# Four graph layers on one core: layer 2's edge records in rows of 512 bytes instead of 264, and a smaller fill of their table

## The chip, the cores and the metric

One of the cores of a Trainium2 chip runs the whole program; the other cores are idle. The metric is the device time of one execution in microseconds. The kernel before was timed three times; beside that there is one profiled execution, from which every duration below is taken.

## The reference

Four graph layers run one after the other on 3125 nodes of 256 features and 53125 edges (25000 random ones, the same reversed, and a loop on each node), sorted by their second endpoint. Each layer is `x = x + layer(relu(layernorm(x)))`:

- layer 0: for each edge, a two-layer perceptron on both endpoints' features and the 64 edge attributes, summed by endpoint; then an update perceptron and a norm;
- layer 1: attention of 4 heads over the edges of a node, with a 64-wide vector for each of 64 edge types, softmax by node;
- layer 2: attention of 8 heads, with `key = k[src] + edge_attr @ We`. Here the softmax runs over all edges at once, and the sum goes to the endpoint by which the edges are *not* sorted:

```python
dst = edge_index[0]
src = edge_index[1]
e = (edge_attr @ We + be).reshape(-1, H, C)
key_j = k[src] + e
alpha = (q[dst] * key_j).sum(-1) / math.sqrt(C)
alpha = jax.nn.softmax(alpha, axis=0)
out = v[src] * alpha[:, :, None]
out = jax.ops.segment_sum(out, dst, num_segments=n)
```

- layer 3: single-head attention with a loop on each node, softmax by node, then a gated cell.

Everything is float32.

## The kernel before

**Stages.** `prelude` builds lists: it counts the edges of each node, ranks the nodes by degree, writes layer 0's table `s_l0_src` (`a_d`, L366) and computes, for every edge, a place in layer 2's table (`t.row2`, L555). At its end a flag says whether the inputs fit the fixed sizes; `tile_gnn_kernel` loads it on every engine and runs `by_slots` where they fit and another function, `by_blocks`, where they don't. `by_slots` then does layer 0 (tile pools `s_e0`), layer 1 (`s_e1`), layer 2 (`s_e2`), the node work before layer 3 (`s_n3`) and layer 3 (`s_e3`). Nodes go in 25 blocks of 128.

**Transfers by index.** Rows of DRAM tables are fetched and stored by indirect DMAs on GpSimd's (POOL's) queue, one index for each of 128 partitions. All go through `Kit.gather` (L154) and `Kit.scatter` (L158); `Kit.queued` keeps their order on POOL as written. The views of the profile tell them apart by the tile: `gt` is layer 0's, `kv<-s_l_kv` layer 1's, `kv<-s_l_rows` layer 2's, `xg` layer 3's; `st` and `s_nodes` belong to the lists, and `out_dram` is the final store, whose last one has 53 rows.

**The records.** Layer 2 needs the edges by their *other* endpoint, in 25 blocks of 128 sources. A block has room for 18 x 128 edges (`TILES`; the last one 8 x 128). For each edge a record is written to its place in the DRAM table `s_src_records` (`ss`): 64 attributes, the offset of the first endpoint's row, and the source's number within its block, 66 floats. The edges are taken 125 at a time, one for each of 125 partitions, in 425 scatters. `loaded` (L588) fetches the attributes for five scatters into one of two buffers `rec`, `filled` writes the two other columns on VectorE (DVE, L592 and L593), and `scatter_src` issues the scatter. These 425 steps are strewn between the gathers of other layers: one after each pair of `gt` gathers of layer 0 from the second block of nodes on, 25 after that, and two after each group of up to four gathers of layer 1.

Places that no edge takes must hold a source number of -1. So the whole table is filled beforehand, on SP's queue, from a constant `sfill`:

```python
for i in range(40):
    nc.sync.dma_start(ss[i * 11 * P:(i + 1) * 11 * P, :].rearrange("(p r) c -> p (r c)", p=P),
                      sfill.rearrange("p r c -> p (r c)"))
```

Behind it on SP's queue stand the stores of `a_d` (L366).

**Layer 2** loads one block of records at a time (`opened`, L1180), into one of two buffers `srec`; each partition reads its 18 records as one run. DVE copies out the row offsets (`dst`, L1183), the source numbers (L1185) and their negatives (L1187), and ScalarE the attributes (L1210). The offsets are the indices of the gathers of `kv`, issued eight pairs of tiles ahead (`fetched`). Two transposed weights of layer 3 are prepared at the start of the same stage, through the same PSUM bank as the first block's attributes (L1156 to L1161).

**What orders the work.** Layer 0 runs on a hand-made clock of ticks, layers 1 to 3 as generators that are stepped in turn. Engines run their own instructions in order; a recording layer puts in the waits. `sync` DMAs go out on SP's queue in the recorded order.

Of the kernel before, what the change touches and what calls it, by code (L numbers as in the profile page):

```python
# [9 lines left out]
F32 = mybir.dt.float32  # L10
# [3 lines left out]
ALU = mybir.AluOpType  # L14
# [4 lines left out]
P = 128  # L19
N = 3125  # L20
NB = 25
# [3 lines left out]
EP, EC = 125, 425  # L25
D = 256
# [4 lines left out]
NT = 440  # L31
# [3 lines left out]
SREC = 66  # L35
# [10 lines left out]
assert HM >= HALF[0]  # L46

TILES = (18,) * (NB - 1) + (8,)
TM = TILES[0]
FR = mybir.dt.float32r  # L50
assert sum(TILES) == NT
XH = 516
KVQ = 1024
XPR = 514
# [188 lines left out]
def prelude(ctx, tc, a, a_d, nodes_d, ss, st_d, flag, t):  # L243
# [3 lines left out]
    nc = tc.nc  # L247
    c = ctx.enter_context(tc.tile_pool(name="pc", bufs=1))
    wk = ctx.enter_context(tc.tile_pool(name="pw", bufs=2))
# [4 lines left out]
    nc.sync.dma_start(dst_i, a["dst"].rearrange("(p c) -> p c", c=EC))  # L254
    xh = c.tile([P, NB, XH], F32, name="xh")
    for b0 in range(0, NB - 1, 6):
# [16 lines left out]
    b1 = k.load_row(c, a["L0_gnn_eb1"], "b1", parts=1)  # L273


    sfill = c.tile([P, 11, SREC], F32, name="sfill")
    nc.gpsimd.memset(sfill, 0.0)
    nc.gpsimd.memset(sfill[:, :, 65:66], -1.0)
    nid = c.tile([P, NB], F32, name="nid")
# [7 lines left out]
    cap = c.tile([P, NB], F32, name="cap")  # L287
    nc.gpsimd.memset(cap, float(P * TM))
    nc.gpsimd.memset(cap[:, NB - 1:NB], float(P * TILES[NB - 1]))
    none = c.tile([1, 512], F32, name="none")  # L290
    nc.gpsimd.memset(none, -BIG)
    last = c.tile([P, NB], F32, name="last")
# [8 lines left out]

    nc.scalar.dma_start(a_d[NP:NP + 1, :], none)

    for i in range(40):
        nc.sync.dma_start(ss[i * 11 * P:(i + 1) * 11 * P, :].rearrange("(p r) c -> p (r c)", p=P),
                          sfill.rearrange("p r c -> p (r c)"))

    both_e = c.tile([EP, EC, 2], I32, name="both_e")
    nc.gpsimd.tensor_copy(both_e[:, :, 0], e_src)
# [161 lines left out]
    pc2, pv = pc3[:, 0:2, :], pc3[0:1, 2, :]  # L471
# [8 lines left out]
    nc.vector.tensor_reduce(v2, most, AX.X, ALU.add)  # L480
    over = c.tile([P, NB], F32, name="over")
    nc.vector.tensor_tensor(over, pc2[:, 1, :], cap, ALU.is_gt)
    v3 = c.tile([P, 1], F32, name="v3")
    nc.vector.tensor_reduce(v3, over, AX.X, ALU.add)
    nc.tensor.matmul(pv[:, 0:1], v1, k.ones[:EP, 0:1], start=True, stop=False)
# [65 lines left out]
    step = wk.tile([EP, EC], F32, name="step", tag="edge", bufs=4)  # L551
    nc.vector.tensor_scalar(step, eq[:, NB - 1, :], float(TILES[NB - 1] - TM), float(TM), op0=ALU.mult, op1=ALU.add)
    nc.vector.tensor_tensor(step, step, pa_i, ALU.mult)
    nc.vector.tensor_tensor(step, step, pj_i, ALU.add)
    nc.vector.scalar_tensor_tensor(t.row2, hs, float(P * TM), step, op0=ALU.mult, op1=ALU.add)  # L555
    nc.vector.tensor_scalar(t.dst_e, dst_i, float(KVQ), None, op0=ALU.mult)
# [3 lines left out]
def by_slots(ctx, tc, a, out, a_d, nodes_d, ss, t):  # L560
    nc = tc.nc
# [17 lines left out]
    srcb, ai, row2, dst_e, srcl_e = t.srcb, t.ai, t.row2, t.dst_e, t.srcl_e  # L579
    attr = a["edge_attr_64"].rearrange("(p c) k -> p c k", c=EC)  # L580
    CH = 5
    recs = ctx.enter_context(tc.tile_pool(name="s_recs", bufs=2))
    done = [0]

    def loaded(c):

        rec = recs.tile([EP, CH, SREC], F32, name="rec")
        nc.sync.dma_start(rec[:, :, 0:64], attr[:, c:c + CH, :])  # L588
        return rec

    def filled(c, rec):
        nc.vector.tensor_copy(rec[:, :, 64], dst_e[:, c:c + CH])  # L592
        nc.vector.tensor_copy(rec[:, :, 65], srcl_e[:, c:c + CH])  # L593
# [3 lines left out]
    def scatter_src(n):  # L597

        for _ in range(n):
            c = done[0]  # L600
            if c == EC:
                return
            c0 = c - c % CH
            if c == 0:
                rec_of[0] = loaded(0)
                filled(0, rec_of[0])
            if c % CH == 1 and c0 + CH < EC:
                rec_of[c0 + CH] = loaded(c0 + CH)
            if c % CH == 3 and c0 + CH < EC:
                filled(c0 + CH, rec_of[c0 + CH])  # L610
            k.scatter(ss, row2[:, c:c + 1], rec_of[c0][:, c % CH, :], "src_records")
            done[0] += 1


    qpool = ctx.enter_context(tc.tile_pool(name="s_q", bufs=1))
    qtab = qpool.tile([P, NB, D], F32, name="qtab", tag="qtab")
    with tc.tile_pool(name="s_e0", bufs=2) as wk, tc.tile_pool(name="s_e0w", bufs=1) as w, \
            tc.tile_pool(name="s_e0p", bufs=2, space=PSUM) as ps:
        w1b = k.load_w(w, a["L0_gnn_eW1"][D:2 * D, :], "w1b")
# [302 lines left out]
        for i in range(-9, len(pairs)):  # L922
            if i >= 0:
                b, s = pairs[i]
# [24 lines left out]
    with tc.tile_pool(name="s_e1", bufs=2) as wk, tc.tile_pool(name="s_e1w", bufs=1) as w, \  # L949
# [144 lines left out]
        def step(ns, nl):  # L1094

            for todo, n in ((soon, ns), (calm, nl)):
                for _ in range(n):
                    if todo and next(todo[0], todo) is todo:
                        todo.pop(0)
            for t in list(late1):  # L1100
                t[0] -= 1
                if t[0] <= 0:
                    late1.remove(t)
                    t[1]()
# [17 lines left out]
        while soon or calm or late1:  # L1122
            step(1, 1)
    scatter_src(EC)

# [17 lines left out]
    with tc.tile_pool(name="s_e2", bufs=2) as wk, tc.tile_pool(name="s_e2w", bufs=1) as w, \  # L1145
# [28 lines left out]
        def opened(b):  # L1174

            o = Block()
            o.b, o.n = b, TILES[b]
            r0 = b * P * TM
            o.rec = wk.tile([P, TM, SREC], F32, name="srec")
            nc.sync.dma_start(o.rec[:, 0:o.n, :].rearrange("p j c -> p (j c)"),  # L1180
                              ss[r0:r0 + o.n * P, :].rearrange("(p j) c -> p (j c)", j=o.n))
            o.dst = wk.tile([P, TM], I32, name="dst2")
            nc.vector.tensor_copy(o.dst[:, 0:o.n], o.rec[:, 0:o.n, 64])  # L1183
            o.slb = wk.tile([P, TM], BF, name="slb")
            nc.vector.tensor_copy(o.slb[:, 0:o.n], o.rec[:, 0:o.n, 65])  # L1185
            o.nsl = wk.tile([P, TM], F32, name="nsl")
            nc.vector.tensor_scalar(o.nsl[:, 0:o.n], o.rec[:, 0:o.n, 65], -1.0, None, op0=ALU.mult)  # L1187
            o.sc = wk.tile([P, TM, 8], F32, name="sc")
            o.kv, o.oh = [], {}

            qt = wk.tile([P, D], F32, name="qt", bufs=1)
            nc.vector.tensor_scalar(qt.bitcast(I32), q2[:, b, :].bitcast(I32), -4096, None, op0=ALU.bitwise_and)
            o.qh = wk.tile([P, D], FR, name="qh")
            nc.scalar.copy(o.qh, qt)
            o.ql = wk.tile([P, D], FR, name="ql")
            nc.vector.tensor_sub(o.ql, q2[:, b, :], qt)
            return o
# [85 lines left out]

        pairs = [(b, j) for b in range(NB) for j in range(0, TILES[b], 2)]
        AHEAD = 8
        blocks = {0: opened(0)}
        for b, j in pairs[:AHEAD]:
            fetched(blocks[b], j)
        ready = turned(blocks[0], 0)
        soon = []  # L1290
        for i, (b, j) in enumerate(pairs):
            o = blocks[b]
            if j == 2 and b + 1 < NB:
                blocks[b + 1] = opened(b + 1)
            if j == 4:

                nc.sync.dma_start(q2[:, b, :], kvq_d[b * P:(b + 1) * P, 768:KVQ])
            eat, oht = ready if j % T6 == 0 else (eat, oht)
            scored(o, j, eat, oht, j % T6 // 2)
            if j % T6 == 2 or (j % T6 == 0 and j + 2 == o.n):  # L1300
                j2 = j - j % T6 + T6
                if j2 < o.n:
                    ready = turned(o, j2)
                elif b + 1 < NB:
                    ready = turned(blocks[b + 1], 0)
            for g in list(soon):
                if next(g, soon) is soon:
                    soon.remove(g)
            if j + 2 == o.n:
                soon.append(weighed(o))  # L1310
            if i + AHEAD < len(pairs):
                b2_, jn = pairs[i + AHEAD]
                fetched(blocks[b2_], jn)
# [1015 lines left out]
def kernel(tc: tile.TileContext, a: dict, out: bass.AP):  # L2329
    nc = tc.nc  # L2330
    a_d = nc.dram_tensor("s_l0_src", [NP + 1, 512], F32, kind="Internal").ap()
    nodes_d = nc.dram_tensor("s_nodes", [NP, XH], F32, kind="Internal").ap()
    ss = nc.dram_tensor("s_src_records", [NT * P, SREC], F32, kind="Internal").ap()
    st_d = nc.dram_tensor("s_src_type", [2 * E], I32, kind="Internal").ap()
    with tc.tile_pool(name="flags", bufs=1) as flags:
        flag = flags.tile([1, 1], I32, name="flag")
        with tc.tile_pool(name="keep", bufs=1) as keep:
            t = Lists(keep)
            prelude(tc, a, a_d, nodes_d, ss, st_d, flag, t)
            _, v = nc.values_load_multi_w_load_instructions(  # L2340
                flag, engines=[ET.PE, ET.DVE, ET.Activation, ET.Pool, ET.SP], min_val=0, max_val=1,
                skip_runtime_bounds_check_because="a comparison's result")
            with tc.If(v[0] == 1):
                by_slots(tc, a, out, a_d, nodes_d, ss, t)
        with tc.If(v[0] == 0):
            by_blocks(tc, a, out)
# [31 lines left out]
```

## Time and profile before

| | us |
|---|---|
| median of 3 runs | 3944.12 (3943.7 to 3950.05) |
| the profiled execution | 3928.64 |
| its span, first to last instruction | 3926.8 |
| PE, DVE, ACT, POOL busy | 2369.8, 2388.1, 1092.7, 2576.2 |
| the 425 record scatters on POOL | 526.6 busy, 1239 ns mean |

The page gives for each engine its busy time; a share of the whole span is a mean over stages that have different limits. A line of a group or of a tile names the source line, the engine, the operation, `out<-in`, the count and the time. A line of waits reads "engine line `<-` what it waited for: us in all, times, longest". In the table of stretches each line is one stretch of the span. "Issue" is time in which an engine waited for nothing that the profile shows. The profiled execution lies 0.4% below the median of the runs, so differences are taken within it.

### The profile page before, as it was taken

The page shows a single profiled execution, that of the slowest core. Times are in us where ns is not written, and L with a number is a line of the kernel's source. Part 1 is how long each engine was busy: PE and PEld are TensorE (multiplying, and loading weights), DVE is VectorE, ACT ScalarE, POOL GpSimd, SP SyncE. Part 2 cuts the span into 40 slices and gives each one's busy share as a digit, 9 for nine tenths or more (in the row PEclk, how much of TensorE's full clock was granted, in tenths as well). Part 3 has the DMA queues.
Part 4 walks back from the last instruction along what each step waited for, and adds up shares of the span by engine and source line. Part 5 has one row for each costly group of instructions (what it writes and reads, how often), then busy time and mean ns, then how long its engine had stood idle before and what let it go on. Part 6 is the DMA issues. An engine that isn't in the chain of part 4 may idle for free. (4 is left out here: it accounts for less than half of the span.)

```text
span 3926.8 us, 32540 instructions
## 1 busy us (share of the span) xinstructions
PE 2369.8 (60%) x9174; PEld 1477.2 (38%) x9174; DVE 2388.1 (61%) x4836; ACT 1092.7 (28%) x2294; POOL 2576.2 (66%) x2497
## 2 busy tenths in 40 slices
PE   5726688878887725354656467699889931121223
PEld 4313244434443424343444355466666630010111
DVE  5646557656575345565656677688989943444444
ACT  1111112212221121121212222566766621011222
POOL 3447777777777067777777763576776626666765
PEclk9868889889898956566667578799999965555556
DMA  6345556566564154555555563666666533333332
GB/s 217 125 140 170 157 155 186 160 175 171 164 177 126 61 169 136 142 154 156 160 148 170 159 187 126 223 209 198 211 208 205 165 106 94 97 92 96 103 100 76
DMA packets 295839, 595.89 MB, mean 152 GB/s; under 512 B 113501, under 2 KB 154508, under 8 KB 295650
## 3 DMA queue, kind: packets, MB, share of 16 engines
q0 software_dynamic: 163616, 472.86, 40.7%
q1 hardware_dynamic: 131512, 119.79, 10.2%
q8 instruction: 76, 1.25, 0.1%
q10 hardware_dynamic: 522, 1.06, 0.1%
q14 instruction: 113, 0.93, 0.1%
HBM read 510.85 MB, written 82.21 MB: 151 GB/s over the span
## 5 line engine op out<-in xcount | busy, mean ns | idle before, releaser
L158 POOL DMA_INDIRECT s_src_records<-rec,row x425 | 526.6, 1239 | 135.9 <-issue 121.8
L154 POOL DMA_INDIRECT kv<-s_l_rows,dst x440 | 456.6, 1038 | 208.9 <-issue 71.9
L154 POOL DMA_INDIRECT kv<-s_l_kv,st x439 | 481.7, 1097 | 167.5 <-issue 120.4
L920 PE MATMUL ph<-wm,st 128*128 128x512 f32 x904 | 477.3, 657 | 150.4 <-DVE acc L939 101.5
L154 POOL DMA_INDIRECT gt<-s_l_src,srcb x452 | 433.8, 960 | 168.2 <-issue 106.3
L154 POOL DMA_INDIRECT xg<-s_l_rows,src x439 | 430.8, 981 | 133.7 <-issue 133.7
L986 PE MATMUL pk<-rel,toh 64*128 64x64 f32 x878 | 183.6, 374 | 367.9 <-DVE mk L988 248.8
L134 PE MATMUL pt<-ident,hb 128*128 128x128 f32 x50 | 17.0, 442 | 555.5 <-ACT hb L1428 555.5
L934 DVE TENSOR_TENSOR ph<-gt,ph 128x1024 f32<-128x1024 f32 x226 | 276.7, 1225 | 122.9 <-PE ph L920 96.3
L988 DVE TENSOR_TENSOR mk<-kv,pk 128x1024 f32<-128x1024 f32 (+3 forms) x119 | 135.2, 1136 | 344.8 <-DMA kv<-s_l_kv,st 330.0
L986 PEld LDWEIGHTS pk<-rel,toh 64*128 64x128 f32 x878 | 165.9, 279 | 401.2 <-issue 348.3
L920 PEld LDWEIGHTS ph<-wm,st 128*128 128x128 f32 x904 | 177.9, 209 | 363.4 <-issue 296.3
L1027 PE MATMUL acc<-kv,ident 128*128 128x256 f32 x878 | 241.6, 442 | 62.3 <-DVE kv L1023 62.3
L981 ACT ACTIVATE toh<-tb,negp 64x512 f32<-64x512 f32 (+3 forms) x119 | 81.9, 688 | 693.3 <-PE pk L986 643.3
L1279 PE MATMUL pg<-kv,oh 128*128 128x256 f32 x880 | 248.8, 408 | 3.7 <-DVE kv L1276 3.4
L939 DVE SCALAR_TENSOR_TENSOR acc<-ph,acc 128x1024 f32<-128x1024 f32 x201 | 245.2, 1220 | 3.6
L1027 PEld LDWEIGHTS acc<-kv,ident 128*128 128x128 f32 x878 | 195.6, 226 | 102.0 <-DVE kv L1023 67.8
L134 PEld LDWEIGHTS pt<-ident,hb 128*128 128x128 f32 x50 | 7.2, 202 | 583.2 <-ACT hb L1428 583.2
L1464 DVE TENSOR_SCALAR sc<-xg,own 128x4 f32<-128x4 f32 (+3 forms) x119 | 30.7, 258 | 322.0 <-DMA xg<-s_l_rows,src 314.8
L1421 DVE SCALAR_TENSOR_TENSOR acc<-xg,sc,acc 128x256 f32<-128x256 f32 x439 | 210.9, 484 | 7.9
L1234 PE MATMUL pk<-we,eat 64*128 64x256 f32 x880 | 162.0, 441 | 45.4 <-DVE mk L1240 43.4
L1240 DVE TENSOR_TENSOR mk<-kv,pk 128x512 f32<-128x512 f32 x220 | 149.6, 680 | 44.2 <-DMA kv<-s_l_rows,dst 38.7
(373 smaller groups left out, 5275.2 us busy)
## 6 DMA issues: line engine op xcount, KB each, us to landing
s_src_records<-sfill SPq DMA_DIRECT2D x40, 363.0 KB
srec<-s_src_records SPq DMA_DIRECT2D x24, 594.0 KB
rec<-in_edge_attr_dram SPq DMA_DIRECT2D x85, 156.2 KB
tb<-s_slot_types SPq DMA_DIRECT2D x101, 128.0 KB
gt<-s_l_src,srcb POOLq DMA_INDIRECT x452, 3.5
kv<-s_l_rows,dst POOLq DMA_INDIRECT x440, 3.8
kv<-s_l_kv,st POOLq DMA_INDIRECT x439, 4.0
xg<-s_l_rows,src POOLq DMA_INDIRECT x439, 2.8
```

The source lines that it names most:

```text
L154: self.queued(lambda: self.nc.gpsimd.indirect_dma_start(out=to, out_offset=None, in_=table, in_offset=bass.IndirectOffsetOnAxis(ap=index, ...
L158: st = self.queued(lambda: self.nc.gpsimd.indirect_dma_start(out=table, out_offset=bass.IndirectOffsetOnAxis(ap=index, axis=0), in_=rows, ...
L920: nc.tensor.matmul(ph[:, h, :], stat[h][:, s % 4, :], ms[b][h], start=True, stop=True)
L934: nc.vector.tensor_add(ph, gt, ph)
L939: nc.vector.scalar_tensor_tensor(accs[b], ph, 0.0, accs[b], op0=ALU.max, op1=ALU.add)
L986: nc.tensor.matmul(pk[:, q, :], toh[:, q, :], rel, start=True, stop=True)
L988: nc.vector.tensor_tensor(mk[:, 0:n].rearrange("p s (h d) -> p s h d", h=4), kv[:, 0:n, 0:D].rearrange("p s (h d) -> p s h d", h=4), pk[:, ...
L1027: nc.tensor.matmul(acc, ident, v[:, q, :], start=(s0 + q == 0), stop=(s0 + q == C - 1))
L1234: nc.tensor.matmul(pk[:, i, :], eat[i * 64:(i + 1) * 64, q, :], we[i * 64:(i + 1) * 64, :], start=True, stop=True)
L1240: nc.vector.tensor_add(mk, o.kv[j // 2][:, :, 0:D], pk)
L1279: nc.tensor.matmul(pg, oh[:, j % T6 + i, :], v[:, i, :], start=(j + i == 0), stop=(j + i == n - 1))
L1421: nc.vector.scalar_tensor_tensor(acc, xgs[q // U3][:, q % U3, 0:D], s[:, q:q + 1], acc, op0=ALU.mult, op1=ALU.add)
```

## The change

A record becomes 128 floats, 512 bytes, of which the last 62 are zeros. The two record buffers become two named tiles whose unused columns are cleared once at the start of `by_slots`; they are given back after the last scatter, ahead of layer 2. The block loads of layer 2 take the wider rows. The fill covers only the last three of each block's 18 (the last block's 8) places of every partition, in three DMAs, and a new test makes a block with fewer edges than the unfilled places hold (15 x 128, in the last block 5 x 128) a violation, which clears the flag. In the inputs a block of sources has 2089 to 2233 edges, the last one 881.

```diff
+FULL = (15,) * (NB - 1) + (5,)
+SW = 128
...
-    sfill = c.tile([P, 11, SREC], F32, name="sfill")
+    sfill = c.tile([P, 3, SW], F32, name="sfill")
...
+    low = c.tile([P, NB], F32, name="low")
+    nc.gpsimd.memset(low, float(P * FULL[0]))
+    nc.gpsimd.memset(low[:, NB - 1:NB], float(P * FULL[NB - 1]))
...
-    for i in range(40):
-        nc.sync.dma_start(ss[i * 11 * P:(i + 1) * 11 * P, :].rearrange("(p r) c -> p (r c)", p=P),
-                          sfill.rearrange("p r c -> p (r c)"))
+    for b0, b1_ in ((0, 12), (12, NB - 1), (NB - 1, NB)):
+        n = TILES[b0]
+        r0 = b0 * P * TM
+        nc.sync.dma_start(ss[r0:r0 + (b1_ - b0) * P * n, :].rearrange("(b p j) c -> p b (j c)", p=P, j=n)
+                          [:, :, FULL[b0] * SW:n * SW],
+                          sfill.rearrange("p r c -> p (r c)")[:, None, :].to_broadcast([P, b1_ - b0, 3 * SW]))
...
     nc.vector.tensor_tensor(over, pc2[:, 1, :], cap, ALU.is_gt)
+    nc.vector.tensor_tensor(low, low, pc2[:, 1, :], ALU.is_gt)
+    nc.vector.tensor_add(over, over, low)
...
-    recs = ctx.enter_context(tc.tile_pool(name="s_recs", bufs=2))
+    qpool = ctx.enter_context(tc.tile_pool(name="s_q", bufs=1))
+    qtab = qpool.tile([P, NB, D], F32, name="qtab", tag="qtab")
+    begun = ExitStack()
+    recs = begun.enter_context(tc.tile_pool(name="s_recs", bufs=1))
+    ring_ = [recs.tile([EP, CH, SW], F32, name=f"rec{i}") for i in range(2)]
+    for rec in ring_:
+        nc.vector.memset(rec[:, :, SREC:SW], 0.0)
...
-        rec = recs.tile([EP, CH, SREC], F32, name="rec")
+        rec = ring_[c // CH % 2]
...
     scatter_src(EC)
+    begun.close()
...
-            o.rec = wk.tile([P, TM, SREC], F32, name="srec")
+            o.rec = wk.tile([P, TM, SW], F32, name="srec")
...
-    ss = nc.dram_tensor("s_src_records", [NT * P, SREC], F32, kind="Internal").ap()
+    ss = nc.dram_tensor("s_src_records", [NT * P, SW], F32, kind="Internal").ap()
```

In the two programs' lists of instructions POOL has the same order but for its memsets, and DVE the same but for the two operations of the new test, the two clearings, and the first record columns, which are written earlier. On SP the fill's 37 stores are gone, and in layer 2 the load of the second block stands behind two loads of weights instead of in front of them. PE and ScalarE have small exchanges of neighbours in the lists' stage and at the start of layer 2.

## The prediction

> **What bounds the kernel now.** I read the page's busy row first. No engine passes 66% of the span, so the average says little and the change has to be priced stage by stage. I cut the span where the names of GpSimd's (POOL's) transfers change: lists up to 237 us, layer 0 (`gt` gathers) 314 to 1236, layer 1 (`kv<-s_l_kv`) 1391 to 2255 with its tail to 2467, layer 2 (`kv<-s_l_rows`) 2467 to 3123, layer 3 (`xg`) from 3206. The table of stretches (columns: stretch, its length, busy us and count for each engine, clock, DMA share, GB/s) then answers for each:
>
> ```profile
> 314.00:1236.00 922.00, 739.88 (x2123) 366.21 (x2123) 574.88 (x782) 191.26 (x390) 708.24 (x684) 0.89 0.59 167
> 1391.00:2255.00 864.00, 440.11 (x1630) 346.75 (x1630) 498.05 (x791) 180.03 (x286) 648.80 (x565) 0.64 0.55 157
> 2467.00:3123.00 656.00, 579.62 (x3309) 407.62 (x3309) 575.97 (x1151) 440.93 (x1005) 455.73 (x440) 0.96 0.65 207
> ```
>
> POOL is busy 708 of 922 us in layer 0, and its waits there say why it is not 922: after each of its 684 transfers stand about 0.3 us "issue" in which it waits for nobody. The groups of layer 0 on POOL give 60.6 + 96.6 + 11.9 + 4.6 = 174 us of that, so 882 of 922 us are POOL going as fast as it can. In layer 1 it is 649 + 155 of 864. Both stages that carry the scatter of records are therefore set by POOL's time per transfer, not by bytes: the DMA engines stand at 0.59 and 0.55. Layer 2, which loads the records, is different: PE 580 and DVE 576 of 656 us, POOL has room.
>
> So three prices matter: POOL's time for one scatter, what waits for its landing, and the block loads of layer 2. The next rows are from the views of single tiles (form, count, minimum/median/maximum in ns):
>
> ```profile
> L158 POOL DMA_INDIRECT s_src_records<-rec,row x425: 1172/1210/2279, 314.6 to 2254.2; - x142
> L154 POOL DMA_INDIRECT st<-s_src_type,off_i x25: 940/944/11131, 172.2 to 213.4; - x25
> L158 POOL DMA_INDIRECT s_nodes<-xh,rank_i x25: 956/960/4613, 130.7 to 164.7; - x25
> L158 POOL DMA_INDIRECT s_l_rows<-row,nid_i x25: 950/987/1890, 1748.3 to 2457.4; - x25
> 3918.40 1.57 POOL L158 DMA_INDIRECT out_dram<-gg,nid_i  x1 [7.03 <-issue]
> ```
>
> The record scatter costs 1.21 us where the others cost 0.94 to 0.99. Is that its short row (264 bytes) or its 125 rows instead of 128? `st` moves 72 to 288 bytes a row, 128 rows, and costs 0.944. `s_l_rows` moves 4096 bytes a row, 128 rows, and costs 0.987. The last line is the final store, 53 rows of 1024 bytes: 1.57. The price follows the number of rows, not their length, and the change keeps 125.
>
> **The change part by part.** The sum is made against the profiled execution, 3928.64 us (span 3926.8); it lies 15.5 us (0.4%) under the median 3944.12, and I carry the difference over to the median.
>
> *The scatter, 425 on POOL.* Row 264 to 512 bytes. By length alone, from 944 (at most 288 bytes) to 987 (4096): 43 ns over 3808 bytes, so 248 bytes are 3 ns, x 425 = 1.2 us. The bounds: a gain of 1210 - 960 = 250 ns each if shortness were the cause, 399 of them in layers 0 and 1, -100 us; a loss of the whole 43 ns each, 425 x 0.043 = +18 us. I take +1, nearest to `st`, whose rows are the only others that short.
>
> Here two rules of the Trainium skill pull apart, both on the page DMA: Bandwidth & Descriptors. "Specifications" says that a transfer under 512 bytes makes the DMA engine read, modify and write; if that were in the 1.21 us, the estimate would be the -100 above. "Why a DMA increments its semaphore by 16 and not by 1" speaks against the change: a transfer runs on the largest number of engines up to 16 that divides its outer dimension, so 128 rows get 16 engines of 8 rows, 125 get 5 of 25, and 53 get one. That orders 0.96, 1.21 and 1.57 as the rows do, and a wider row leaves 125 at 5; by it the sum stays.
>
> *The landing of the scatter.* Issue to landing is 3.1 us now, 3.8 for `s_l_rows` with its 4096-byte rows. In proportion 248 of 3832 bytes add 0.05 us; 0.7 us is the upper bound, and 0.2 us below nothing (`s_nodes` lands in 2.9). Two things wait for it: SP, which reloads the buffer (L588; behind it on SP's queue stand layer 0's node loads and stores and layer 1's `tb` loads, and ScalarE waited for that once, 22.1 us), and DVE, which writes two columns of the next buffer at L592:
>
> ```profile
> DVE rec L592 <- DMA s_src_records<-rec,row: 234.0, 42, 14.6
> DVE rec L592 <- DMA s_src_records<-rec,row: 192.9, 31, 14.6
> POOL gt L154 <- DVE ph L934: 13.1, 31, 2.0
> POOL kv L154 <- PE acc L1027: 34.0, 11, 13.4
> ```
>
> (whole span, layer 0, then what POOL waits for in layers 0 and 1). DVE stands up to 14.6 us there with the adds of layer 0 queued behind, and PE behind them, yet POOL waited only 13.1 us in all for those adds: five pairs of `gt` buffers are 5 x 2 x 1.25 us of gathers plus five scatters of 1.5, 20 us, and they cover it. 42 x 0.05 = 2 us more of DVE's wait, hidden; +0 on the path. With the 0.7: 29 us of DVE, which the cover still holds in layer 0; in layer 1 the 11 waits on PE could each grow, +8 us.
>
> *The fill.* 40 stores of 363 KB become three of 2.4, 2.4 and 0.2 MB, 4.9 MB instead of 14.5. SP issues them from 18.6 to 71.6 us with only the `a_d` stores behind, and these wait for ScalarE's copies (first at 69.9). The compute that follows does not wait:
>
> ```profile
> 66.10:97.40 31.30, 31.30 (x244) 21.89 (x245) 5.57 (x34) 3.98 (x9) 0.00 (x0) 0.78 0.42 158
> 97.40:130.70 33.30, 33.30 (x123) 14.64 (x123) 18.00 (x57) 7.40 (x17) 0.85 (x1) 0.90 0.15 56
> ```
>
> PE is busy for every microsecond from the second half of the counting to the ranks, so 10 MB less beside it free nothing: 0. Below 66 us DVE counts on one load that is in at 7.5 us. POOL's smaller memsets and its two new ones (0.1 us each) end before its 91.7 us wait at L523.
>
> *The new check* is two DVE operations of 128x25, 0.18 us each (L482's row), ahead of L519, which DVE runs back to back: +0.4 us on the path. The two clearings of the record ring run at 237 us, ahead of DVE's 22.65 us wait for `qc`: at 0.6 us each (a 125x425 operation, L553) they hide; uncovered they would be +1.2.
>
> *The loads of layer 2* grow from 594 to 1152 KB. Block 4's load is issued at 2531.27 and its first reader (L1183) runs at 2566.22, 35 us later, and later blocks alike: covered by a whole block. Added traffic is 24 x 558 KB = 13.4 MB; at 207 GB/s for a share of 0.65 that is 42 us of a full fabric in 656, share 0.65 to 0.71. DVE's strided reads keep their 18 elements. Only the start is bare:
>
> ```profile
> 2474.95 0.18 DVE L1183 CAST dst<-srec 128x18 int32<-128x18 f32 x1 [7.71 <-DMA srec<-s_src_records]
> 2476.48 0.18 DVE L1183 CAST dst<-srec 128x18 int32<-128x18 f32 x1 [0.98 <-DMA srec<-s_src_records]
> ```
>
> Two loads issued back to back land 1.53 us apart, so one of double size costs about +1.5 before the first gather. On SP the second block's load also slips behind two weight loads, and the later weight loads behind it; what waits for them is the transposes that share a bank with the first block's. I allow 0 to +4 and take +1.5; a gain is excluded, as nothing queued ahead of the first load shrinks.
>
> Sum: 1 + 0 + 0 + 0.4 + 1.5 = about +3 us; the profiled execution would be 3931, the median 3947.
>
> **The rivals.**
> 1. *Short rows are the reason for 1.21 us.* Then each scatter falls to about 0.96, and layers 0 and 1 lose 100 us (PE's 740 and DVE's 575 us leave room): 3844. Half that if only part of it is length: 3894. `st` at 0.944 and the last store at 1.57 speak against it; for it, that `st` is a gather and no scatter is as short.
> 2. *Scatters land sooner*, by the 0.2 us to `s_nodes`, or DMA queues clear, and block edges in layer 1 (77 waits of DVE on `kv`, 305 us) shorten by 0.2 each: -15, 3929. Against it: POOL, not landing, sets the pace.
> 3. *The wider scatter delays gathers behind it* (slower). In layer 1 two scatters precede each four gathers, and DVE's product waits for the fourth. If landing grows by 0.3 to 0.7 us, 77 waits grow by 23 to 54 us on DVE; it decides once DVE's lag exceeds the nine `kv` buffers, as it already does at the 11 waits on PE. Priced at half, +25: 3969. Against it: DVE is busy 498 of 864 us and can catch up.
> 4. *It doesn't do what it says*: a block of sources with fewer than 1920 edges (the last: 640) would send all to the other branch, a different program that no run here shows. The inputs' counts are 2089 to 2233, and 881 in the last, so this is all but excluded.
>
> **How the numbers follow.** A measurement of this kernel can tell about 0.2%, 8 us, from no change (the three runs span 6). The forecast has 0.56, its unknowns (0 to +18, mostly under +5) staying within 8 us; rival 1 has 0.10, rival 2 0.09, rival 3 and the upper bound of the scatter's price 0.24, rival 4 0.01. Faster: 0.10 + 0.09 = 0.19; same 0.56; slower 0.24 + 0.01 = 0.25. The range must reach into rivals 2 and 3 until at most 0.2 is out: 3929 leaves out rival 1 and a little of 2, 3968 the far part of 3. The forecast's own range is 3940 to 3955.
>
> **What would show it.** Right: the scatter's median still 1.20 to 1.22 us; layers 0 and 1 within 5 us of 922 and 864; degree counting ends near 97 us; the first L1183 one to four microseconds later against the last `s_l_rows` scatter. Wrong: a scatter under 1.1 us (rival 1), L592's 234 us well up together with POOL waits on DVE or PE (rival 3), or layer 2's 656 us changed beyond its start.

## The result, and the profile after

| | before | after |
|---|---|---|
| median | 3945.41 us (4 runs, 3943.7 to 3950.05) | 3983.09 us (4 runs, 3980.38 to 3984.94) |
| the profiled execution | 3928.64 | 3980.38 |
| its span | 3926.8 | 3978.5 |

The changed kernel takes 1.0093 times as long, with a 95% interval of 1.0076 to 1.0111: slower by 37.7 us between the medians. The forecast, 3947 with a range of 3929 to 3968, was wrong. The two profiled executions lie 51.7 us apart, because the one of before is 0.4% under its median; the account below is made between these two, so some 14 us of its difference belong to that one execution of before.

Line numbers of the changed kernel are 2 higher than before at the top of the file and 15 higher in layer 2. The stages first, in the table of stretches of the changed kernel (columns: stretch, its length, busy us and count of PE, PEld, DVE, ACT and POOL, granted clock, DMA share, GB/s); the stretches follow the same first and last transfers of each layer:

```profile
314.00:1236.00 922.00, 729.24 (x2120) 360.88 (x2119) 573.00 (x781) 191.26 (x389) 708.74 (x683) 0.90 0.61 173
1391.00:2258.00 867.00, 443.17 (x1630) 347.77 (x1630) 497.80 (x793) 180.24 (x286) 653.54 (x565) 0.64 0.57 163
2470.00:3175.00 705.00, 608.04 (x3307) 429.79 (x3308) 578.78 (x1150) 440.92 (x1005) 456.46 (x439) 0.90 0.64 212
```

Layers 0 and 1 stand within 3 us of what they were (922 and 864). Layer 2 was 656 us and is 705. Its DMA share did not rise from 0.65 to 0.71, as added bytes in an unchanged time would have made it; the time rose instead. And the granted clock fell from 0.96 to 0.90.

The rows on which the rest of the sum stood (the scatter in the view of its table, DVE's wait for its landing in the waits of the whole span, the first two readers of layer 2's loads in the order of time):

```profile
L160 POOL DMA_INDIRECT s_src_records<-rec,row x425: 1172/1211/3403, 312.7 to 2257.7; - x142
```

```profile
DVE rec L608 <- DMA s_src_records<-rec,row: 239.0, 41, 16.8
```

```profile
2479.45 0.18 DVE L1198 CAST dst<-srec 128x18 int32<-128x18 f32 x1 [9.42 <-DMA srec<-s_src_records]
2484.11 0.18 DVE L1198 CAST dst<-srec 128x18 int32<-128x18 f32 x1 [4.10 <-DMA srec<-s_src_records]
```

The scatter's median is 1211 ns for 1210. The wait for its landing is 239.0 for 234.0 us. From the last `s_l_rows` scatter (2457.4 before, 2459.9 after) to layer 2's first cast are 17.6 us before and 19.6 now. The second cast is 4.7 us behind the first, where it was 1.5.

**Where layer 2 loses.** One block of sources follows another at the cast of L1183, now L1198, and a block is counted here from one cast to the next. The program records a block's casts behind the first pair of the block before it, so the last of the nine products `mk` ahead of a cast is that of a first pair (`j == 0` in the code). The median distance of two casts is 26.2 us before and 28.5 after. Over the 21 blocks from the fourth cast to the last it is 556.6 and 600.0 us. The whole difference of 51.7 us is 2.5 ahead of layer 2, 2.0 at its start, 4.4 in its first three blocks, 43.4 in these 21, and -0.6 behind them. (Two other traces, of `e14` and `e5` below, are 563.3 and 596.9 us in the 21 blocks, 33.6 apart, so in an ordinary execution the loss there may be nearer to 34.) DVE runs the same 48 instructions in the same order in each block, so their starts can be laid beside each other. In two places only do the starts drift apart by more than a microsecond or so in all. Between the cast and `zall` (L1266, now L1281) the sum over the 21 blocks is 167.0 us before and 188.2 after (+21.2). The wait ahead of the block's last product `mk`, taken as the distance of the starts beyond the 0.6 us that it has without a wait, is 35.8 and 58.1 us (+22.3). Together they are 43.5.

*The second place first.* Some of DVE's waits from 2526 to 3137 us, before (first fence) and after:

```profile
DVE mk L1240 <- DMA kv<-s_l_rows,dst: 38.7, 28, 3.4
DVE mall L1262 <- PE pe L1260: 4.3, 7, 0.9
DVE zall L1266 <- ACT sc L1264: 2.8, 7, 0.8
DVE m L1258 <- PE pe L1255: 1.6, 2, 0.9
```

```profile
DVE mk L1255 <- DMA kv<-s_l_rows,dst: 61.3, 27, 4.0
DVE mall L1277 <- PE pe L1275: 11.0, 20, 1.0
DVE m L1273 <- PE pe L1270: 6.8, 9, 0.8
DVE zall L1281 <- ACT sc L1279: 6.5, 20, 0.3
```

The wait for `kv` is one wait a block, of 1.7 us before and 2.8 after (medians). It stands a few microseconds behind SP's issue of a block load, 17.5 us into a block before and 18.5 after (medians). Three stretches around one such issue, in the tables of before (issue at 2798.2) and after (2826.4):

```profile
2795.00:2799.00 4.00, 4.00 (x23) 2.62 (x21) 3.68 (x8) 2.81 (x8) 3.09 (x4) 1.00 0.50 159
2799.00:2803.00 4.00, 3.70 (x21) 2.76 (x20) 3.31 (x6) 2.73 (x6) 3.09 (x4) 1.00 0.94 304
2803.00:2807.00 4.00, 2.54 (x18) 1.79 (x16) 3.12 (x8) 2.76 (x7) 3.09 (x4) 1.00 0.76 251
```

```profile
2822.00:2827.50 5.50, 5.33 (x32) 3.66 (x30) 5.18 (x11) 3.05 (x8) 4.29 (x4) 1.00 0.59 165
2827.50:2833.50 6.00, 3.84 (x20) 2.77 (x20) 3.23 (x7) 4.55 (x12) 4.71 (x5) 1.00 0.94 358
2833.50:2836.00 2.50, 1.82 (x10) 1.39 (x11) 2.50 (x5) 0.69 (x1) 1.90 (x2) 0.81 0.81 270
```

The last two columns are to be read. The share of 0.65 is a mean of stretches of 0.5 to 0.8 and of one near 0.94 behind each load; that full stretch is about 4 us long before and 6 after. Gathers that are in flight in it land late. The view of `kv` gives the time from issue to landing: 3.9 us in the median for the gathers at 2783 to 2793 before and 3.7 at 2809 to 2819 after, well ahead of the load; for the four issued within 2.4 us of the load's own issue, before and after:

```profile
DMA to landing us min/median/max: 4.3/4.5/4.9
```

```profile
DMA to landing us min/median/max: 4.7/5.6/6.2
```

These are not chosen blocks: over 20 blocks, gathers issued 6 to 15 us ahead of a load land after 3.7 us in the median in both kernels, and those issued within 2.5 us of it after 5.0 us before and 6.1 after.

*The first place.* While DVE waits for `kv`, PE waits for DVE. Then this follows, on PE (order of time, after; rows are left out at the dots) and, around the start of the block before that one, in the granted clock:

```profile
2831.28 0.28 PE L1253 MATMUL pq<-ql,oht 128*128 128x256 f32 x1
2834.18 0.70 PE L1249 MATMUL pk<-we,eat 64*128 64x256 f32 x4 [2.62 <-DVE mk L1255]
...
2836.62 1.99 PE L1294 MATMUL pg<-kv,oh 128*128 128x256 f32 x4
...
2839.34 1.13 PE L1294 MATMUL pg<-kv,oh 128*128 128x256 f32 x4
```

```profile
2806.40:2811.20 4.80, 4.80 (x19) 3.36 (x19) 4.04 (x12) 0.74 (x2) 0.86 (x1) 0.51 0.35 120
2811.20:2830.00 18.80, 18.09 (x111) 13.13 (x109) 17.35 (x33) 14.30 (x33) 13.09 (x14) 1.00 0.57 178
```

Four `pg` matmuls take 1.99 us where they take 1.13 a little later, and a stretch of 4.8 us at the start of a block runs at 0.51 of the clock. The trace dates each spell of half clock; around these blocks it is 3.4 or 6.8 us long. Its price shows when the blocks of both kernels are sorted by the half clock between their cast and `zall`. Where there is none (15 blocks before, one after), `zall` comes 7.6 us after the cast; with 1.6 to 3.4 us of half clock, 8.3 to 8.6 us after it; with 4.3 to 4.8 us, 9.6 to 9.9. Before, 6 blocks of 21 start with half clock; after, 20 of 21.

### The profile page after: what moved, and what is told of

Its sections match the earlier page's. It is cut to its first block, busy times and chain, and to the rows that moved or that the text cites. A ratio compares the mean times of both kernels' runs of the same rounds, so it can differ in the third digit from the quotient of the medians.

```text
span 3978.5 us, 32474 instructions
## 1 busy us (share of the span) xinstructions
PE 2387.9 (60%) x9174; PEld 1493.9 (38%) x9174; DVE 2390.2 (60%) x4840; ACT 1092.6 (27%) x2294; POOL 2580.1 (65%) x2499
## 5 line engine op out<-in xcount | busy, mean ns | idle before, releaser
L1294 PE MATMUL pg<-kv,oh 128*128 128x256 f32 x880 | 258.5, 421 | 3.7 <-DVE kv L1291 3.4
L1249 PE MATMUL pk<-we,eat 64*128 64x256 f32 x880 | 170.7, 463 | 63.1 <-DVE mk L1255 62.2
```

Of the source, the lines that this page charges most:

```text
L1249: nc.tensor.matmul(pk[:, i, :], eat[i * 64:(i + 1) * 64, q, :], we[i * 64:(i + 1) * 64, :], start=True, stop=True)
L1294: nc.tensor.matmul(pg, oh[:, j % T6 + i, :], v[:, i, :], start=(j + i == 0), stop=(j + i == n - 1))
```

## The experiments

Each kernel here was timed beside the kernel before on the same chip. The chip of `e1` to `e4` ran the kernel before at 4206 us; the chips of the others ran it at 3938 to 3944, so ratios are compared. The theory: **A**, the 1152 KB of a load take the DMA engines from the gathers beside it. Rivals: **B**, the engines' time goes by pieces, not bytes; **C**, another part of the change (stride on chip, order, fill, test, record tiles); **D**, layer 2 is bound by bytes wherever the burst stands. **A'**: the half clock has a price of its own; **D'**: once the wait is cured, DVE's and PE's own work and order set the pace.

**One part at a time.** `e1` narrows the load in the changed kernel:

```diff
-            nc.sync.dma_start(o.rec[:, 0:o.n, :].rearrange("p j c -> p (j c)"),
-                              ss[r0:r0 + o.n * P, :].rearrange("(p j) c -> p (j c)", j=o.n))
+            nc.sync.dma_start(o.rec[:, 0:o.n, 0:SREC],
+                              ss[r0:r0 + o.n * P, :].rearrange("(p j) c -> p j c", j=o.n)[:, :, 0:SREC])
```

> The changed kernel, but each block load of layer 2 fetches 66 of the 128 floats of a record, into the same tile (rows still 512 bytes apart in DRAM and on chip). Bytes per load are 594 KB again, in pieces of 264 bytes instead of one run for each partition. Theory A (the burst of 1152 KB takes the DMA engines from the gathers, in bytes): the wait of DVE's L1255 on kv falls from 61 to about 40 us, the block period from 28.5 to about 26.2 us, time 3945 to 3950. Rival B (the engines' time goes by pieces, not bytes: 2304 pieces of 264 bytes are no cheaper than 128 runs of 9216): 3980 or more. Rival C (layer 2's wider stride on chip or its order of instructions slows the engines themselves): 3980, with the kv wait back at 40.

`e2` lengthens it in the kernel before; what is read beyond the block's own records is not used:

```diff
+            run = TM * 128 if b < NB - 1 else o.n * SREC
+            wide = wk.tile([P, TM * 128], F32, name="srec")
+            o.rec = wide[:, 0:TM * SREC].rearrange("p (j c) -> p j c", c=SREC)
+            nc.sync.dma_start(wide[:, 0:run], bass.AP(tensor=ss.tensor, offset=ss[r0:r0 + 1, :].offset,
+                                                      ap=[[o.n * SREC, P], [1, run]]))
```

> The kernel before with records of 264 bytes everywhere, but each block load of layer 2 fetches 9216 bytes for each partition instead of 4752 (the surplus is not read). Nothing else of the change. Theory A (bytes of the load): the whole loss comes back, 3980 to 3988, block period 28.5, DVE's wait on kv near 61 us, half-clock spells of PE in nearly every block. Rival C (stride, order, or the other parts of the change): 3945 to 3950.

`e3` keeps the changed kernel but for `SW = SREC` (and the clearing, which has nothing left to clear):

> The changed kernel with records of 264 bytes: the small fill, the new test, the two named record tiles given back ahead of layer 2, all as changed; only the row width is undone. Theory A: these parts cost the few microseconds of the prediction's sum, 3944 to 3949. Rival C (fill, test, ring or order carry the loss): 3970 to 3985. A gain of the small fill would show as 3935 to 3940.

Ratios to the kernel before on that slower chip: `e1` 1.0002 (0.9984 to 1.0020), `e2` 1.0063 (1.0038 to 1.0087) and `e3` 0.9996 (0.9975 to 1.0018). All three were repeated on the faster chips, with the changed kernel itself as measure:

> The changed kernel once more, unaltered, as the measure for the others of this call on the same chip. Expected: 1.0093 times the kernel before, as first measured (1.0076 to 1.0111); on a chip that runs the kernel before at about 4200 us the loss may be nearer to the 1.0063 that the kernel with longer block loads alone showed there.

> The kernel before with 264-byte records whose block loads of layer 2 fetch 9216 bytes for each partition, again, because the first chip ran the kernel before at 4206 us instead of 3945. Theory A: the whole loss of the change, ratio 1.009 to 1.012, block period 28.3 to 28.6, wait of DVE's L1242 on kv near 60 us. Rival C (stride, order, the rest of the change): 1.000 to 1.002.

> The changed kernel whose block loads fetch 66 of the 128 floats of a record, again, for the same reason. Theory A in bytes: ratio 1.000 to 1.002, period near 26.2. Rival B in pieces (2304 of 264 bytes instead of 128 of 9216): 1.005 or more.

> The changed kernel with records of 264 bytes (small fill, new test and record tiles kept), again. Theory A: 0.998 to 1.002 of the kernel before; any gain of the small fill would be below 0.998; anything above 1.003 is a cost that the load of layer 2 doesn't explain.

| | ratio to before | interval |
|---|---|---|
| the changed kernel (e5) | 1.0109 | 1.0092 to 1.0126 |
| before, with longer loads only (e10) | 1.0130 | 1.0105 to 1.0156 |
| changed, with 264 of 512 bytes loaded (e11) | 1.0045 | 1.0027 to 1.0064 |
| changed, with records of 264 bytes (e14) | 0.9994 | 0.9982 to 1.0005 |

So the length of the load alone brings the whole loss (`e10` even a little more than its forecast of at most 1.012). The rest of the change, in `e14` without the wider scatter and the two clearings, costs nothing measurable; the small fill brings no gain either. The scatter itself shows no price in the trace of the changed kernel (1211 ns, layers 0 and 1). Rival C falls. In `e10` DVE's wait for `kv` at 2526 to 3083 us is 64.6 us (57.1 in the changed kernel, 38.3 before) and the median block 28.75 us. Rival B is half right: 594 KB in pieces of 264 bytes cost 0.45%, more than the same bytes in runs of 4752, though less than 1152 KB in runs of 9216. The DMA view shows the same in the engines' own time. These are the rows of the queue that holds the block loads, in 20 blocks each (packets, MB, share of 16 engines over the stretch): before at 2540.3:3072.2, after at 2549.2:3124.4, `e11` at 2554.3:3104.3:

```profile
q1 hardware_dynamic: 5760, 14.45, 8.8%
q1 hardware_dynamic: 5760, 25.56, 12.8%
q1 hardware_dynamic: 48000, 14.45, 12.1%
```

Share times stretch is 47 us before, 74 after and 67 in `e11`. The added bytes thus take 27 us of all 16 engines in 20 blocks, 1.3 us a block, and the short pieces take 20 us more without a byte more. `e11` keeps the stride of 512 bytes on chip, whose own effect on time is not parted from the pieces by it; its loss lies in layer 2 (27.4 us a block). On the slower chip the same kernel had shown no cost.

**Another place for the burst.** `e6` is the changed kernel, `e7` the kernel before, each with

```diff
-            nc.vector.tensor_scalar(o.nsl[:, 0:o.n], o.rec[:, 0:o.n, 65], -1.0, None, op0=ALU.mult)
+            nc.vector.tensor_scalar(o.nsl[:, 0:o.n], o.slb[:, 0:o.n], -1.0, None, op0=ALU.mult)
```

which frees `srec` earlier. `e8` is the kernel before with `bufs=18` for `kv2`.

> The changed kernel with one operand exchanged: nsl (L1202) is made from slb instead of from the record tile, so that the tile is free, and the next block's load is issued, after the last copy of attributes (about 12 us into a block) instead of after L1202 (18.3 us). Same bytes, same instructions. Theory A (the loss is a collision: the burst stands ahead of just those gathers whose product DVE reads next, at 26.5 us into the block): six microseconds earlier the burst meets gathers with slack, the waits of L1255 on kv fall below 40 us, period from 28.5 to 25.5 to 27, time at or below the kernel before. Rival D (layer 2 is bound by bytes, 207 GB/s before and 207 after): the period stays at 28.5, ratio to before 1.007 to 1.010, wherever the burst stands.

> The same exchange in the kernel before (264-byte records). Theory A: its own wait of 1.6 us per block on kv, behind the load of 594 KB, goes too: 22 blocks, up to 36 us, and some of the six spells of half clock: ratio 0.990 to 0.997. Rival D: 1.000.

> The kernel before with 18 buffers of kv2 instead of 16: the gathers of a block's first pair no longer wait for the product of the third pair of two blocks before, so they are issued earlier than the block load. Theory A: as in the exchange of operands, 0.990 to 0.997. Rival D: 1.000; a rise above 1.002 would say that earlier gathers only meet the load at another place.

Measured: `e6` 1.0050 (1.0036 to 1.0063), `e7` 0.9946 (0.9931 to 0.9961) and `e8` 0.9932 (0.9915 to 0.9949). In `e6` and `e7` the load is issued at 11.45 us into a block, as meant. Theory A's forecast for `e6` failed in size: DVE's wait for `kv` at 2526 to 3083 us is 51.5 us, where less than 40 had been expected, and the time is not back at the kernel before. The wait moved with the burst, to the block's seventh product:

```profile
2818.03 0.69 DVE L1255 TENSOR_TENSOR mk<-kv,pk 128x512 f32<-128x512 f32 x1 [2.11 <-DMA kv<-s_l_rows,dst]
```

(order of time of `e6`). Every block's start is at full clock there, though, with `zall` 7.5 to 7.7 us behind the cast in all 21 blocks, although the loads are as long as in the changed kernel. The half clock is not gone: 68 us of spells in the 21 blocks, where the changed kernel has 98, now follow the wait at the seventh product, and DVE waits 18.2 us for `pk` of PE at 2526 to 3083 us, where it waited 1.3. The gain of 0.6% on `e5` is what is left of both. Between `e6` and `e7` lies 1.0%, about as much as between `e5` and the kernel before (1.1%): at either place the added bytes cost their time. D's forecast of an unchanged period failed (28.3 to 27.1 us), but neither of the two places that were tried lets a block take 558 KB more for nothing.

**The half clock by itself.** `e4` puts idle matmuls where PE waits:

```diff
             scored(o, j, eat, oht, j % T6 // 2)
+            if j == 0 and b > 0:
+                more = ps.tile([P, 4, P], F32, name="pb", bufs=1)
+                for _ in range(48):
+                    nc.tensor.matmul(more[:, 0, :], identb, identb, start=True, stop=True)
```

> The changed kernel with 48 idle matmuls of 128x128 (bf16, result not read) behind the first pair of each block from the second on, where PE otherwise waits 2 to 4 us for DVE, which waits for kv. Theory A' (a wait of over about 2 us makes the granted clock of TensorE fall to half for 3.4 or 6.8 us, and that costs another 1.0 us in each block beside the 1.9 of the longer wait): the clock stays at 1.0 in layer 2, the m<-pe and mall<-pe waits at the start of a block vanish, period 28.5 to about 27.5, time 3955 to 3965. Rival (the half clock is only a sign of the wait and hidden by it): 3980, or 3990 to 4010 if the idle matmuls are themselves on the path.

1.0077 (1.0049 to 1.0106) on the slower chip, no better than `e2` there. With 32 instead of 48, on a faster chip:

> The changed kernel with 32 idle matmuls of 128x128 (bf16, result not read) for each block from the second on, where PE waits for DVE's L1255; 48 on the other chip were on the path. They fill 1.8 of PE's 2.5 to 3 us of waiting and shorten nothing else. Theory A' (the half clock that follows the long wait costs 1.0 us a block, at m<-pe, mall<-pe and zall): period 28.4 to about 27.4, 0.994 to 0.996 of the changed kernel, ratio to before 1.005 to 1.007. Rival (the half clock is hidden): 1.010 or more.

0.9959 (0.9946 to 0.9973): 1.5%, some 58 us, faster than the changed kernel (`e5`), far more than the 21 us at which the clock was priced, and faster than either forecast. The clock from 2526 to 3083 us is 1.00, but the added instructions had also changed the recorded order of the engines' work: DVE's order in a block is another one, POOL's pauses of over 0.5 us are 56 us in 21 blocks instead of 104, and DVE's wait for `kv` is 18.4 us. Two things changed at once, so `e12` does not decide A'. Three attempts to part them follow; "block" in the second is that of the code, whose last product stands just ahead of the one that waits:

```diff
# e13: 32 matmuls of one column
+                    nc.tensor.matmul(more[:, 0, 0:1], identb, identb[:, 0:1], start=True, stop=True)
# e17, behind the last product of a block but the last (e18: range(1))
             nc.vector.tensor_mul(mk, mk, pq)
+            if j + 2 == o.n and o.b < NB - 1:
+                more = ps.tile([P, 4, P], F32, name="pb", bufs=1)
+                for _ in range(20):
+                    nc.tensor.matmul(more[:, 0, 0:16], ident, mk[:, 0, 0:16], start=True, stop=True)
```

> The changed kernel with 32 idle matmuls of one column (128x1, each with a weight load of 128x128) for each block from the second on, behind its first pair. DVE's order and the gathers' stay those of the changed kernel. Theory A': if weight loads keep the granted clock, the half-clock spells at the start of the blocks go, zall comes at 7.6 us into a block instead of 8.4 to 9.9, and the wait on kv stays: ratio to before 1.004 to 1.007. If they don't keep it: 1.010 to 1.012, which says that most of e12's gain was its order.

> The changed kernel with 20 idle matmuls in each block (16 columns of float32, result not read), which take the product of the block's last pair as operand and so can only start where PE's wait for L1255 starts. Theory A': they keep the granted clock; zall comes at 7.6 us into a block, the wait on kv stays near 55 us; against e18 the time falls by 0.7 to 1.2 us a block, 15 to 25 us, 0.994 to 0.996 of e18. Rival (half clock is hidden, or such matmuls don't keep the clock): the same as e18 or slower.

> As e17 with one idle matmul instead of 20: the same order of DVE in a block without work for PE in the wait. Theory A': ratio to the kernel before near that of the changed kernel, 1.008 to 1.013, half clock at the start of nearly every block.

`e13` gave 1.0123 (1.0107 to 1.0139): its matmuls ran ahead of the wait, around the seventh product, and left the wait empty; nothing follows for the clock. `e18` gave 1.0171 (1.0148 to 1.0194), above its forecast: its order of DVE's instructions is not that of the changed kernel, and what its further 0.6% are was not found. `e17` gave 1.0332 (1.0312 to 1.0352), slower than `e18` and not faster: each float32 matmul became two passes (960 for 24 blocks), the fill was longer than the wait (5.3 us against 3.5 in one block), and the clock was at half all the same, 157 us of spells in 21 blocks. A' is therefore shown by the sorting of blocks within the traces and by the starts of the blocks in `e6`, not by a kernel that removes the half clock alone; what work would keep the clock in that wait stays open.

**Together.** Both remedies in the kernel before, then the kernel before with `e12`'s lines, then all three:

> The kernel before with both remedies: nsl made from slb (load issued 6 us earlier) and 18 kv2 buffers. Each alone gave 0.995 and 0.993. Theory A: the load's burst meets gathers that are issued 0.7 us earlier than with 16 buffers, so the wait of 1.2 us left at the last product goes and the one that the early load brought at the seventh shrinks: 0.988 to 0.993. Rival D' (the remedies cure the same wait, and what is left is set by DVE and PE, 25 us a block): 0.993, no better than the better of the two.

> The kernel before (264-byte records) with e12's 32 idle matmuls, which bring e12's order of instructions. Theory A (the loads' burst costs through the gathers' slack): in this order the gathers run without a gap and the load of 594 KB is hidden, so 0.990 to 0.996. If the burst's size still costs as in the order of before, the step from e12 is 0.009: 0.986 to 0.988. If e12's order hides any load: 0.995 to 0.997, no better than e12 with 512-byte rows.

> As e15, with nsl made from slb and 18 kv2 buffers. Theory A: what is left of the wait on kv behind the load shrinks further: 0.985 to 0.992. Rival D' (DVE's 22.9 us and PE's 22.8 us of work in a block and their order set the pace by now): as e15, and as e9's 0.993.

`e9` 0.9930 (0.9909 to 0.9950), `e15` 0.9887 (0.9873 to 0.9902) and `e16` 0.9887 (0.9872 to 0.9901). Two remedies together do no more than one (0.9932 in `e8`), and nothing on top of `e15`: they cure the same wait, as rival D' said, although 0.993 is also the end of theory A's range for `e9`. `e15`, 3894.9 us, is 1.1% faster than the kernel before and 2.2% than the changed one. DVE's largest wait there and the stretch 2526:3083:

```profile
DVE mk L1240 <- DMA kv<-s_l_rows,dst: 7.6, 7, 1.9
```

```profile
2526.00:3083.00 557.00, 549.67 (x3765) 402.80 (x3764) 539.16 (x1066) 393.87 (x927) 397.68 (x400) 1.00 0.67 216
```

DVE is busy 539 of 557 us. Even in this order the long load costs: 0.9959 with 512-byte rows (`e12`), 0.9887 with 264. This lies between the forecasts for `e15`: the order hides a part of the burst, not all.

## Why the prediction was wrong

- **The bound of each stage** was read for layers 0 and 1 in a way that nothing here contradicts: their DMA share rose from 0.59 and 0.55 to 0.61 and 0.57, their time by 0 and 3 us. For layer 2 it was read from busy sums (PE 580, DVE 576 of 656 us, "POOL has room"); the 1.7 us that DVE waited for `kv` in each block were in the waits of before, and the prediction does not use them.
- **The scatter** (+1): right. 1211 ns; rows of 512 bytes are neither faster nor slower, and rival 1 is out.
- **Its landing** (0): 3.4 us for 3.1, DVE's wait +5, hidden as said. Rivals 2 and 3 (-15 and +25 us) are out: up to the last scatter ahead of layer 2 only 2.5 us moved.
- **The fill** (0) and **the test** (+0.4): together 0.9994 of the time, 0.9982 to 1.0005 (`e14`), so nothing that can be told from 0. The clearings are not in `e14`; they are within the 2.5 us just named.
- **The start of layer 2** (+1.5): 2.0 us.
- **The loads of layer 2**: this step failed. It asked whether the load's own reader would wait ("35 us later, and later blocks alike: covered by a whole block"), and that was true. The price had been worked out in the next sentence, "42 us of a full fabric in 656, share 0.65 to 0.71", and was then set to nothing, although the only reason in the text is a share that stays under one. Measured: 43.4 us in 21 blocks (33.6 between `e14` and `e5`). A mean share of 0.65 hid 4 us in each block at 0.94, and the gathers caught in them are those that DVE reads next: 16 buffers were too little reserve, since a gather is issued only when the last reader of its buffer is done (in the kernel before, two more buffers gave 0.7%, `e8`). The Trainium skill says on the page DMA: Bandwidth & Descriptors, section "Issuing engines are not separate DMA queues", that transfers from SP and from GpSimd run on the same 16 engines and interleave. The landings of 5.6 us for the gathers issued beside the load, 3.7 well ahead of it, agree; the prediction had not weighed it. No rival held this; rival 3 looked for a transfer that delays gathers in the scatters of layer 1, not in the loads of layer 2.
- That the sum of 42 comes so near is chance. It went by a full rate worked out from the mean share; the added packets took 1.3 us of all engines a block, 32 us in 24 blocks. And of the 43.4 us lost, 22.3 are waits for `kv` and 21.2 the half clock that follows them; the prediction had neither.

The text had named "layer 2's 656 us changed beyond its start" as what would prove it wrong, and that is what came.

## What to carry to other kernels

A load that is issued a whole block ahead is covered against its own latency, not against the transfers beside it: price its bytes at the full rate of the DMA engines, and look in stretches of a few microseconds behind its issue whether they are full there and who reads what is then in flight. (Here that price was 1.3 us a block, and the loss 1.6 to 2.1.) Where a stage is a closed loop (a transfer is issued when a buffer comes free), there may be no reserve to absorb a burst, as here, and an added microsecond comes once in every turn. Padding rows for the sake of a store multiplies what every later load moves; here the store gained nothing.

## What the runs showed of the hardware

- A short wait of PE can cost twice. Between 2540 and 3060 us of the changed kernel PE stood idle for 2.1 to 3.9 us 18 times, and each time a spell of half clock, 3.4 or 6.8 us long, began in the last 0.7 us of the wait or up to 1.4 us behind it. In the same stretch of the kernel before, five of 17 idle times of 1.3 to 1.9 us were followed by one, a single one of 2.2 us was not, one of 3.3 us was. So length alone does not decide: in `e6`, `e7`, `e13` and `e14` too a wait of 2.2 to 2.4 us passed once without a spell. The Trainium skill, on the page TensorE: Matmul & The Clock Gate, section "HAM oscillation — how this bites in real kernels", warns of gaps over about 3.4 us. The measurement decides here: 16 of the 18 gaps were shorter.
- Added idle matmuls made a kernel faster by 1.1% (`e15`). They kept the clock and changed the recorded order at once. Most of it must be the order: the 21 blocks fell from 556.6 to 523.6 us, and the half clock at the start of six blocks of the kernel before had cost 7 us (`zall` 167.0 us behind the casts in all, 160 at full clock).
- One chip ran the same program at 4206 us; elsewhere it took 3938 to 3945.
